# A four-layer kernel on one core: scatters moved behind a branch, gate weights loaded in attention, routing in pairs, folds reordered

## The chip, the cores and the metric

The program runs on one core of a Trainium2 chip. A core has a matrix engine (TensorE, here PE, with its weight loads PEld), a vector engine (VectorE, DVE), a scalar engine (ScalarE, ACT), a general engine (GpSimd, POOL) and an engine that issues transfers (SyncE, SP). Each follows its own list of instructions in order and waits on semaphores for the others. Transfers are issued on the queues of SP, ACT and POOL and run on 16 DMA engines that all queues share. The metric is the device time of one execution in microseconds (us). Before the change it is 3014.77 us, the median of three runs (3004.94 to 3015.94).

## The reference

The input is two sequences of 1024 tokens with 512 features. Four layers follow one another, each after a layer normalisation and added to its input:

```
x = x + attention(norm(x))        # 16 heads of 32, causal
x = x + experts(norm(x))          # 32 experts of inner width 192, the best 8 a token
x = x + state_space(norm(x))      # 16 heads, chunks of 64
x = x + feed_forward(norm(x))     # width 1376, weights looked up in a table of 16 values

# experts:
sel_w, sel_e = top_k(x @ gate_w.T, 8)
sel_w = softmax(sel_w)
h = silu(x @ w_gate[e].T) * (x @ w_up[e].T)
out = sum over the 8 of sel_w * (h @ w_down[e].T)
```

## The kernel before

All is done in 32-bit floats. Tokens stand in 16 blocks of 128 (`x_sb`), blocks 0 to 7 of sequence 0 and 8 to 15 of sequence 1.

**Attention** works in eight groups of four heads: groups 0 to 3 of sequence 0, groups 4 to 7 of sequence 1. Within a group, `scores` makes the score tiles of one block of keys, ACT takes their exponentials (`pT`), POOL masks the diagonal tiles, `values` multiplies by the values. Beside it, `maxima` makes the scores of the *next* group a first time, for their largest values only; `fold` turns these maxima (a DVE reduction into `nm`, four PE transposes `nm_ps`, ACT copies into spare rows of the queries) so that later scores come out with the maximum subtracted. `project_qk` makes the queries and keys of the group after the next, in four steps of 8 products each, evicted by DVE and ACT in turn. In this stage the order on PE, DVE and ACT is as written by hand: the generators are advanced one step at a time in `group`. The other queues, and everything outside attention, are ordered by a planner that goes by the order in which the program is traced and by its own idea of when things are ready. At the end of a group come one step of the projection, what is left of the maxima, the first fold, the last values, two steps of the projection, the second fold, the last step.

`normalise` makes a sequence's normalised features, and has POOL add the output bias to `x_sb`. At the start (`first_groups`) the first half of sequence 0 is normalised and projected before the second half. `clear_some` sends zeros to the scatter's destination during attention.

**Routing** (`_Router`): `route` takes some blocks, writes them to the accumulator, normalises, multiplies by the router, takes the best eight, and works out for each token and place a row number in `rows`, where each expert has 640 rows. `send` scatters the blocks' normalised rows to `rows`, one indirect DMA on POOL for each block and place. Places are ordered so that the first place holds the token's highest expert. A token that finds its expert full is handled apart: `finish` sets `over` if there is any, all five engines read it, and a branch (`tc.If`) runs `_left_over`. Sequence 0 is routed within attention (`route_first`). Sequence 1 is routed in `route_last`, two groups of four blocks, along with the last output projection: 64 scatters, all of them traced ahead of the branch.

**Experts** (`_sparse_experts`) go from 31 down to 0. `load_rows` fetches an expert's 640 rows, and waits for those places that can hold it (the first place for expert 31, the first two for 30, and so on). Five transposes turn them, `gates` makes 48 products with the gate weights `wgu`, `down` makes up to ten with `wd` and ACT's scaled result `y` (6 buffers) is added to the accumulator by an indirect DMA on POOL (line 988). Beside the experts DVE looks up the feed-forward weights (`_look_up`), and SP fetches the weights of the state space layer (`fetch`). Weights of the experts are loaded two experts ahead (`_expert_weights`); those of the first two are asked for after attention.

The **state space** layer and the **feed-forward** follow; the change doesn't touch them. A table of the former, `tri`, is loaded on ACT's queue (line 1145), and the planner puts that load ahead of ACT's first copies for the experts.

Of the kernel before, what the change touches and what calls it, by code (L numbers as in the profile page):

```python
# [18 lines left out]
P = 128  # L19
# [21 lines left out]
CAPB = 5  # L41
# [60 lines left out]
class _Router:  # L102
# [147 lines left out]
    def send(self, routed, places):  # L250
        tc = self.tc
        blocks, xr, idx = routed
        for k in places:
            for i, blk in enumerate(blocks):
                t = tc.nc.gpsimd.indirect_dma_start(  # L255
                    out=self.rows[:, :],
                    out_offset=bass.IndirectOffsetOnAxis(ap=idx[:, i, k : k + 1], axis=0),
                    in_=xr[i], in_offset=None,
                )
# [24 lines left out]
def _attention(tc, g, x_sb, a, router):  # L284
# [14 lines left out]
    with ExitStack() as ctx:  # L299
# [22 lines left out]

        load_x(range(TBLK // 2))
        load_w("wq", "wq")
        load_w("wk", "wk")
# [7 lines left out]

        bqs = wp.tile([P, NG], F32, tag="bqs", name="bqs")
        nc.vector.tensor_scalar(bqs, bqk[:, 0, :], DH**-0.5, None, ALU.mult)
# [44 lines left out]
        def normalise(b):  # L380

            for grp in range(TBLK // 4):
                blocks = range(b * TBLK + grp * 4, b * TBLK + grp * 4 + 4)
                norms = _norms(nc, g, x_sb, blocks)
                yield
                nc.vector.reciprocal(norms[1], norms[1])
                before = None
                for i, blk in enumerate(blocks):
                    xn = _normed(nc, x_sb, i, blk, norms, rp, ("row", ROW))
                    if before:  # L390
                        _turn(nc, g, *before, xnT, ps_f, "f")
# [27 lines left out]
        def project_qk(i):  # L419
# [4 lines left out]
            for hf in range(2):  # L424
                tok = slice(hf * 512, (hf + 1) * 512)
                for s, (dst, wn) in enumerate(((q, "wq"), (k, "wk"))):
                    pq = ps_f.tile([P, 512], F32, tag="f", name="pq")
                    for cc in range(NCC):
                        nc.tensor.matmul(
                            pq,  # L430
                            lhsT=w[wn][:, cc, gi * P : (gi + 1) * P],
                            rhs=xnT[:, cc, hf * 512 : (hf + 1) * 512],
                            start=cc == 0,
                            stop=cc == NCC - 1,
                        )
# [80 lines left out]
        def fold(i, hf):  # L516
# [8 lines left out]
            )  # L525
            pt = ps_s.tile([P, 4, P], F32, tag="s", name="nm_ps")
# [141 lines left out]
        def route_last(y):  # L668

            sk = ctx.enter_context(tc.tile_pool(name="rt_wk", bufs=1))  # L670
            psum = ctx.enter_context(tc.tile_pool(name="rt_ps", bufs=2, space=PSUM))

# [37 lines left out]
        def first_groups():  # L710


            norm, first = normalise(0), project_qk(0)
            for _ in range(6):
                next(norm)
            for _ in range(2):
                next(first)
                for _ in range(2):
                    next(norm)
            run(norm)  # L720
            run(first)
# [4 lines left out]
            fold(0, 0)  # L726
            run(other)
            fold(0, 1)
            load_w("wo", "wvo")

        def group(i, beside, sending):
# [55 lines left out]
            if follows:  # L787
                fold(i + 1, 1)
# [26 lines left out]
        route_last(y)  # L815
# [40 lines left out]
def _expert_weights(tc, a, pool):  # L856
# [5 lines left out]
    def load(e):  # L862
# [12 lines left out]
        wd = pool.tile([P, 2, D], F32, tag="wd", name="wd", bufs=3)  # L875
        src = a["wd"][e // 2]
        nc.sync.dma_start(out=wd[:, 0, :], in_=src[:, e % 2 * 2, :])
        tail = src[e % 2 * HB : (e % 2 + 1) * HB, 1, :]
        for r in (0, HB):
            nc.sync.dma_start(out=wd[r : r + HB, 1, :], in_=tail)  # L880
        return wgu, wd
# [4 lines left out]
def _sparse_experts(tc, g, a, router, ffn_w, load, loaded, fetch):  # L886
# [8 lines left out]
    with ExitStack() as ctx:  # L895
# [6 lines left out]
        wk = pool("se_wk", 2)  # L902
        ps_g = pool("se_ps_g", 4, PSUM)
# [8 lines left out]
        def load_rows(e):  # L912
            xg = wk.tile([P, CAPB, ROW], F32, tag="xg", name="xg")
            got = nc.sync.dma_start(
                out=xg,
                in_=rows[1 + e * CAP : 1 + (e + 1) * CAP, :].rearrange("(n p) d -> p n d", p=P),
            )

            needed = [s for sent in router.sent for s in chain(*sent[: E - e])]
            for s in needed:  # L920
                _after(tc, got, s)
            tc.declare_no_dep(
                got.ins, group="sent", keep=[s.ins for s in needed],
                reason="the other places hold no row of this expert",
            )
            return xg

# [76 lines left out]
        came = [load_rows(e) for e in order[:2]]  # L1004
# [4 lines left out]
        for n, e in enumerate(order):  # L1009
            wgu, wd = loaded[n]  # L1010
# [16 lines left out]
            if n + 2 < E:  # L1027
                loaded.append(load(order[n + 2]))
# [491 lines left out]
def kernel(ctx: ExitStack, tc: tile.TileContext, a: dict, out: bass.AP):  # L1520
# [26 lines left out]
    with tc.tile_pool(name="tokens", bufs=1, side="right") as tok:  # L1547
        x_sb = tok.tile([P, NBLK, D], F32, tag="x", name="x_sb")
        router = _Router(tc, g, x_sb, a, pool, rows, acc, left, [])
        _attention(tc, g, x_sb, a, router)  # L1550
        ew = first.enter_context(tc.tile_pool(name="se_w", bufs=1, reuse_waits="tile"))
        load = _expert_weights(tc, a, ew)
        loaded = [load(e) for e in (E - 1, E - 2)]
        some = nc.values_load(router.over[0:1, 0:1], min_val=0, max_val=1)
        with tc.If(some > 0):
            _left_over(tc, g, x_sb, a, left, acc[0])

# [22 lines left out]
    _sparse_experts(tc, g, a, router, ffn_w, load, loaded, fetch())  # L1580
# [106 lines left out]
```

## Time and profile before

| what | us |
|---|---|
| median of three runs | 3014.77 |
| the profiled execution | 3022.81 |
| its span, first to last instruction | 3020.7 |
| PE busy in the span | 2787.6 (92%) |
| DVE busy | 1382.0 (46%) |
| ACT busy | 928.1 (31%) |
| POOL busy | 632.6 (21%) |
| last output projection of attention ends | 829.2 |
| first product of the experts starts | 924.8 |

The profile is of one execution. A row of the timeline gives the start and the duration, the engine (a q behind it stands for its queue or sequencer), the line of the kernel, the operation, what it writes and reads, the shape and how many are drawn together, and in brackets how long the engine had been idle and what ended that. A row of the waits has who waited for whom, the total in us, the times and the longest. Starts of PE are measured and its ends are modelled. A row for one tile or line has the least, median and largest duration in ns, and the first and last start.

### The profile page before, as it was taken

The numbers are of one execution on the slowest core, as the hardware profiler recorded it, in microseconds if no ns is written. First come the engines' busy times: TensorE is split into PE (matmuls) and PEld (weight loads), VectorE is DVE, ScalarE is ACT, GpSimd is POOL, SyncE is SP. The second block draws the span as 40 slices with busy tenths as digits, with TensorE's granted clock in tenths as the row PEclk, the third lists the DMA queues.
The fourth block names the chain that finished last, engine by engine and source line by source line (L and its number), as shares of the span: only waits on it lengthen the run. The fifth ranks groups of instructions, "written<-read, shape, count | busy, mean of one in ns | idle before, by whom it ended". The sixth has DMA issues, their size and how long they took to land. (4 is left out here: it accounts for less than half of the span.)

```text
span 3020.7 us, 34117 instructions
## 1 busy us (share of the span) xinstructions
PE 2787.6 (92%) x11848; PEld 1624.7 (54%) x11848; DVE 1382.0 (46%) x3836; ACT 928.1 (31%) x1873; POOL 632.6 (21%) x786
## 2 busy tenths in 40 slices
PE   7998999989917999999999799999999997999999
PEld 3444444444414555555555378777777774444444
DVE  5555543545316999998111135545554454011010
ACT  1344432434302333333333234444444342100010
POOL 3022210423363334333333301101111010000000
PEclk9999999999858999999999889999999997999999
DMA  2466421212278988787877611111111132000000
GB/s 107 121 178 172 148 92 48 72 45 77 95 266 283 255 191 198 187 180 171 185 167 167 108 33 26 40 43 29 42 41 36 30 103 87 0 0 32 20 9 25
DMA packets 237685, 310.31 MB, mean 103 GB/s; under 512 B 60001, under 2 KB 126561, under 8 KB 236481
## 3 DMA queue, kind: packets, MB, share of 16 engines
q1 hardware_dynamic: 202928, 229.53, 24.9%
q0 software_dynamic: 33280, 77.68, 13.1%
q8 instruction: 97, 1.59, 0.2%
q10 hardware_dynamic: 1296, 0.83, 0.1%
q14 instruction: 84, 0.68, 0.1%
HBM read 159.12 MB, written 148.85 MB: 102 GB/s over the span
## 5 line engine op out<-in xcount | busy, mean ns | idle before, releaser
L944 PE MATMUL pg<-xgT,wgu 128*128 128x320 f32 x1536 | 469.2, 450 | 1.5 <-issue 1.5
L988 POOL DMA_INDIRECT acc<-y,tok x160 | 272.7, 1704 | 524.9 <-ACT y L987 364.3
L944 PEld LDWEIGHTS pg<-xgT,wgu 128*128 128x128 f32 x1536 | 285.1, 195 | 171.3 <-issue 61.6
L848 DVE SCALAR_TENSOR_TENSOR acc<-hit,lut,acc 128x688 f32<-128x688 bf16 (+2 forms) x405 | 345.3, 855 | 5.3
L1241 PE MATMUL pf<-xT,win 128*128 128x256 f32 x1024 | 242.5, 385 | 4.7 <-ACT gate L1269 3.9
L490 PE MATMUL sp<-ka,qa 64*128 64x512 f32 (+3 forms) x768 | 209.0, 514 | 6.5 <-DVE mx L511 3.2
L594 ACT ACTIVATE pT<-st 128x512 f32<-128x512 f32 (+3 forms) x384 | 158.2, 498 | 182.2 <-PE st L581 158.9
L1241 PEld LDWEIGHTS pf<-xT,win 128*128 128x128 f32 x1024 | 187.0, 190 | 38.0 <-PE pf L1241 6.0
L581 PE MATMUL st<-qa,ka 64*128 64x512 f32 (+3 forms) x768 | 177.4, 500 | 2.6 <-issue 1.9
L511 DVE TENSOR_REDUCE mx<-sp 128x1 f32<-128x384 f32 (+3 forms) x352 | 167.3, 492 | 16.9 <-PE sp L490 16.7
L1501 PE MATMUL pg<-xT,wg 128*128 128x512 f32 (+1 forms) x352 | 159.1, 595 | 0.0
L1510 DVE TENSOR_TENSOR hT<-s,pu 128x512 f32<-128x512 f32 (+1 forms) x44 | 30.3, 688 | 281.1 <-PE pu L1501 281.1
L1501 PE MATMUL pu<-xT,wu 128*128 128x512 f32 (+1 forms) x352 | 158.2, 592 | 0.0
L598 POOL TENSOR_SCALAR_AFFINE_SELECT pT<-pT 128x128 f32<-128x128 f32 x256 | 83.0, 337 | 347.7 <-ACT pT L594 335.5
L974 PE MATMUL po<-wd,hT 128*128 128x512 f32 x320 | 153.3, 593 | 1.6 <-ACT y L987 1.6
L612 PE MATMUL y<-pT,v 128*64 128x512 f32 (+3 forms) x768 | 149.7, 524 | 3.8 <-issue 2.9
L1483 PE MATMUL po<-wd,hT 128*128 128x512 f32 (+1 forms) x352 | 152.6, 592 | 0.0
L987 ACT ACTIVATE y<-po,rw 128x512 f32<-128x512 f32 x160 | 104.0, 685 | 155.4 <-PE po L981 151.1
L935 PE MATMUL xg_ps<-ident,xg 128*128 128x128 f32 x640 | 98.3, 278 | 57.2 <-issue 57.2
L255 POOL DMA_INDIRECT rows<-row,idx x128 | 126.1, 985 | 111.0 <-issue 71.3
L490 PEld LDWEIGHTS sp<-ka,qa 64*128 64x128 f32 x768 | 91.8, 187 | 94.7 <-issue 50.0
L981 PE MATMUL po<-wd,hU 64*128 64x512 f32 x320 | 126.0, 647 | 16.4 <-DVE hU L961 16.4
(190 smaller groups left out, 3822.9 us busy)
## 6 DMA issues: line engine op xcount, KB each, us to landing
rows<-blank SPq DMA_DIRECT2D x160, 272.5 KB
xg<-rows SPq DMA_DIRECT2D x32, 1362.5 KB
csb<-cs_rows SPq DMA_DIRECT2D x128, 128.0 KB
wgu<-in_wg_dram SPq DMA_DIRECT2D x32, 256.0 KB
wgu<-in_wu_dram SPq DMA_DIRECT2D x32, 256.0 KB
wd<-in_wd_dram SPq DMA_DIRECT2D x32, 256.0 KB
wd<-in_wd_dram SPq DMA_DIRECT2D x64, 128.0 KB
x<-x SPq DMA_DIRECT2D x32, 256.0 KB
```

What stands on the lines that cost most here:

```text
L490: nc.tensor.matmul(sp[hh][:, c0:c1], lhsT=q[half, pr, tb * P : (tb + 1) * P], rhs=k[half, pr, k0 * P : k1 * P], start=True, stop=True,)
L511: nc.vector.tensor_reduce(m[:, n : n + 1], sp[hh][:, c0:c1], AX.X, ALU.max)
L581: nc.tensor.matmul(st[:, c0:], lhsT=k[half, j // 2, kb * P : (kb + 1) * P], rhs=q[half, j // 2, qt * 512 + c0 : (qt + 1) * 512], start=Tru ...
L594: e = nc.scalar.activation(pT[:, c0:], st[:, c0:], AF.Exp)
L612: nc.tensor.matmul(y[j // 2][half, c0:], lhsT=v[:, kb, h // 2, h % 2 : h % 2 + 2, :].rearrange("p k d -> p (k d)"), rhs=ps[j][:, c0:], sta ...
L848: nc.vector.scalar_tensor_tensor(acc, hit, lut[:n, k : k + 1], acc, ALU.mult, ALU.add)
L944: nc.tensor.matmul(pg, lhsT=wgu[:, cc, m * P : (m + 1) * P], rhs=xgT[:, cc, cols], start=cc == 0, stop=cc == NCC - 1,)
L974: nc.tensor.matmul(o, lhsT=hT[:, j * P : (j + 1) * P], rhs=wd[:, 0, :], start=True, stop=False,)
L988: nc.gpsimd.indirect_dma_start(out=acc[turn[0] % 2][:, :], out_offset=bass.IndirectOffsetOnAxis(ap=tok[:, j : j + 1], axis=0), in_=y, in_o ...
L1241: nc.tensor.matmul(pf, lhsT=w[wn][:, cc, c0 : c0 + P], rhs=xT[st][:, cc], start=cc == 0, stop=cc == NCC - 1,)
L1483: nc.tensor.matmul(po, lhsT=hT[:n, fc, j * P : (j + 1) * P], rhs=wd[:n, fc, :], start=fc == 0, stop=fc == NFC - 1,)
L1501: nc.tensor.matmul(dst[:n, :], lhsT=w[:, cc, fc * P : fc * P + n], rhs=xT[:, cc, :], start=cc == 0, stop=cc == NCC - 1,)
```

## The change

- The scatters of sequence 1 are split. Blocks 8 to 11, 12 and 13, and 14 and 15 are routed as three parts (before: two groups of four blocks). Ahead of the branch two, two and one place of them are sent, 8 + 4 + 2 = 14 scatters. `route_last` returns the other 50, which are traced behind the branch, in the order of places.
- The gate weights and the others of an expert are parted. `wgu` tiles (two) are made before attention; there they hold the first 384 columns of `wq` and of `wk`, whose last 128 columns have tiles of their own. From group 6 on, the tiles take the gate weights of experts 31 and 30. `wd` is loaded within `_sparse_experts`.
- The first expert's rows come in five transfers of 128 rows each.
- `fold` becomes a generator with a pause behind its reduction. At the end of a group the rest of the maxima comes first, then the first reduction, a step of the projection, the first transposes, the second reduction, the last values, two steps, the second transposes, the last step.
- At the start all eight blocks of sequence 0 are normalised ahead of the first projection, and the scaling of the query bias (`bqs`) stands behind it. The output bias is added beside group 0 (sequence 0) and group 3 (sequence 1), by POOL.
- In `route_last` the scatters are no longer ordered behind the last mask.

```diff
@@ _Router.send
-                _after(tc, t, self.mask, mybir.DependencyClass.NoSync)
+                if self.mask is not None:
+                    _after(tc, t, self.mask, mybir.DependencyClass.NoSync)
@@ _attention
+        def load_qk(n):
+
+            w[n] = (
+                gates.tile([P, NCC, 2 * I], F32, tag="wgu", name=n, bufs=2),
+                wp.tile([P, NCC, P], F32, tag=n, name=n),
+            )
+            for t, c in zip(w[n], (0, 2 * I)):
+                nc.sync.dma_start(out=t, in_=a[n][:, :, c : c + t.shape[2]])
+
         load_x(range(TBLK // 2))
-        load_w("wq", "wq")
-        load_w("wk", "wk")
+        load_qk("wq")
+        load_qk("wk")
...
@@ normalise
                     before = xn, blk % TBLK
+                    yield
+                _turn(nc, g, *before, xnT, ps_f, "f")
+                yield
+
+        def output_bias(b):
+            for blk in range(b * TBLK, (b + 1) * TBLK):
+                tc.keep_in_program_order(
                     nc.gpsimd.tensor_tensor(
                         x_sb[:, blk, :], x_sb[:, blk, :], bvo[:, 1, :], ALU.add
                     )
-                    yield
-                _turn(nc, g, *before, xnT, ps_f, "f")
+                )
                 yield
@@ fold
                 mxs[i][:, t0 : t0 + 4], AX.X, ALU.max, negate=True,
             )
+            yield
             pt = ps_s.tile([P, 4, P], F32, tag="s", name="nm_ps")
@@ route_last
+            router.mask = None
...
             out = project_out(1, y)
-            routed, routing = [], iter(())
-            for grp in range(2):
-                for _ in range(4):
-                    next(out)
-                    routed += advance(routing)
-                    routed += advance(routing)
-                while len(routed) < grp:
-                    routed += advance(routing)
-                if grp:
-                    run(router.send(routed[0], range(4)))
-                blocks = range(TBLK + grp * 4, TBLK + grp * 4 + 4)
-                routing = router.route(blocks, sk, row_of, bank)
+            active, routed = [], []
+            parts = {3: range(8, 12), 5: range(12, 14), 7: range(14, 16)}
+            places = (2, 2, 1)
+
+            def advance_all():
+                for r in list(active):
+                    done = advance(r)
+                    if done:
+                        active.remove(r)
+                        run(router.send(done[0], range(places[len(routed)])))
+                        routed.extend(done)
+
+            for tb in range(TBLK):
+                next(out)
+                for _ in range(2):
+                    advance_all()
+                if tb in parts:
+                    sk = ctx.enter_context(tc.tile_pool(name=f"rt_wk{tb}", bufs=1))
+                    active.append(router.route(parts[tb], sk, row_of, bank))
             run(out)
-            while len(routed) < 2:
-                routed += advance(routing)
-            run(router.send(routed[1], range(4)))
-            for r in routed:
-                run(router.send(r, range(4, TOPK)))
+            while active:
+                advance_all()
             router.finish(bank)
+            return [
+                (r, [k]) for k in range(TOPK) for r, n in zip(routed, places) if k >= n
+            ]
@@ first_groups
-            norm, first = normalise(0), project_qk(0)
-            for _ in range(6):
-                next(norm)
-            for _ in range(2):
-                next(first)
-                for _ in range(2):
-                    next(norm)
-            run(norm)
-            run(first)
+            run(normalise(0))
+
+            nc.vector.tensor_scalar(bqs, bqk[:, 0, :], DH**-0.5, None, ALU.mult)
+            run(project_qk(0))
@@ group
+            run(more)
+            first, second = (fold(i + 1, hf) if follows else iter(()) for hf in range(2))
+            next(first, None)
             next(ahead, None)
-            run(more)
-            if follows:
-                fold(i + 1, 0)
+            run(first)
+            next(second, None)
             one(len(blocks) - 1)
             for _ in range(2):
                 next(ahead, None)
-            if follows:
-                fold(i + 1, 1)
+            run(second)
             run(ahead)
@@ the loop over groups
-                if i == 2:
+                if i == 0:
+                    beside = output_bias(0)
+                elif i == 2:
                     beside = normalise(1)
+                elif i == 3:
+                    beside = output_bias(1)
+                elif i == 6:
+                    for e in (E - 1, E - 2):
+                        load_gates(e)
@@ _sparse_experts
-        came = [load_rows(e) for e in order[:2]]
+        came = [load_rows(order[0], CAPB)]
+        wds = [load_down(order[0])]
+        came.append(load_rows(order[1]))
+        wds.append(load_down(order[1]))
@@ tile_preln_layers_kernel
-        _attention(tc, g, x_sb, a, router)
-        ew = first.enter_context(tc.tile_pool(name="se_w", bufs=1, reuse_waits="tile"))
-        load = _expert_weights(tc, a, ew)
-        loaded = [load(e) for e in (E - 1, E - 2)]
+        gates = first.enter_context(tc.tile_pool(name="se_w", bufs=1))
+        loaded = {}
+        load_gates = _expert_gates(tc, a, gates, loaded)
+        rest = _attention(tc, g, x_sb, a, router, gates, load_gates)
         some = nc.values_load(router.over[0:1, 0:1], min_val=0, max_val=1)
         with tc.If(some > 0):
             _left_over(tc, g, x_sb, a, left, acc[0])
+        for routed, places in rest:
+            for _ in router.send(routed, places):
+                pass
```

More of the change, by code (lines that the diff above doesn't have):

```diff
@@ L281, in _after, with _attention @@
     )
-def _attention(tc, g, x_sb, a, router):
+def _attention(tc, g, x_sb, a, router, gates, load_gates):
     nc = tc.nc
@@ L334, in _attention @@
         bqs = wp.tile([P, NG], F32, tag="bqs", name="bqs")
-        nc.vector.tensor_scalar(bqs, bqk[:, 0, :], DH**-0.5, None, ALU.mult)
         bvo = wp.tile([P, 2, D], F32, tag="bvo", name="bvo")
@@ L430, in project_qk @@
                             pq,
-                            lhsT=w[wn][:, cc, gi * P : (gi + 1) * P],
+                            lhsT=w[wn][gi // 3][:, cc, gi % 3 * P : (gi % 3 + 1) * P],
                             rhs=xnT[:, cc, hf * 512 : (hf + 1) * 512],
@@ L668, in route_last @@
         def route_last(y):
-            sk = ctx.enter_context(tc.tile_pool(name="rt_wk", bufs=1))
             psum = ctx.enter_context(tc.tile_pool(name="rt_ps", bufs=2, space=PSUM))
+            router.mask = None
             def bank(tag, shape):
@@ L725, in first_groups @@
                     next(other)
-            fold(0, 0)
-            run(other)
-            fold(0, 1)
+            run(fold(0, 0))
+            run(fold(0, 1))
             load_w("wo", "wvo")
@@ L814, in _attention @@
         inner.close()
-        route_last(y)
+        return route_last(y)
 def _look_up(tc, g, a, pool, lut, ffn_w):
@@ L853, in _look_up, with _expert_gates @@
             yield
-def _expert_weights(tc, a, pool):
+def _expert_gates(tc, a, pool, loaded):
     nc = tc.nc
@@ L874, in load, with _sparse_experts @@
             )
[L875 to L881, printed above, removed]
+        loaded[e] = wgu
     return load
-def _sparse_experts(tc, g, a, router, ffn_w, load, loaded, fetch):
+def _sparse_experts(tc, g, a, router, ffn_w, load_gates, loaded, fetch):
     nc = tc.nc
@@ L902, in _sparse_experts @@
         wk = pool("se_wk", 2)
+        dw = pool("se_wd", 3)
         ps_g = pool("se_ps_g", 4, PSUM)
@@ L910, in _sparse_experts, with load_rows, load_down @@
         look_up = _look_up(tc, g, a, lk, lut, ffn_w)
-        def load_rows(e):
+        def load_rows(e, parts=1):
             xg = wk.tile([P, CAPB, ROW], F32, tag="xg", name="xg")
[L914 to L917, printed above, removed]
             needed = [s for sent in router.sent for s in chain(*sent[: E - e])]
[L920 to L925, printed above, removed]
-            return xg
+            src = rows[1 + e * CAP : 1 + (e + 1) * CAP, :].rearrange("(n p) d -> p n d", p=P)
+            for n in range(0, CAPB, CAPB // parts):
+                part = slice(n, n + CAPB // parts)
+                got = nc.sync.dma_start(out=xg[:, part], in_=src[:, part])
+                for s in needed:
+                    _after(tc, got, s)
+                tc.declare_no_dep(
+                    got.ins, group="sent", keep=[s.ins for s in needed],
+                    reason="the other places hold no row of this expert",
+                )
+            return xg
+        def load_down(e):
+            wd = dw.tile([P, 2, D], F32, tag="wd", name="wd")
+            src = a["wd"][e // 2]
+            nc.sync.dma_start(out=wd[:, 0, :], in_=src[:, e % 2 * 2, :])
+            tail = src[e % 2 * HB : (e % 2 + 1) * HB, 1, :]
+            for r in (0, HB):
+                nc.sync.dma_start(out=wd[r : r + HB, 1, :], in_=tail)
+            return wd
         def transpose(xg, t):
@@ L1009, in _sparse_experts @@
         for n, e in enumerate(order):
-            wgu, wd = loaded[n]
+            wgu, wd = loaded[e], wds[n]
             xgT, tok, rw = t
@@ L1027, in _sparse_experts @@
             if n + 2 < E:
-                loaded.append(load(order[n + 2]))
+                load_gates(order[n + 2])
+                wds.append(load_down(order[n + 2]))
                 came.append(load_rows(order[n + 2]))
@@ L1578, in fetch @@
         yield
-    _sparse_experts(tc, g, a, router, ffn_w, load, loaded, fetch())
+    _sparse_experts(tc, g, a, router, ffn_w, load_gates, loaded, fetch())
     first.close()
```

## The prediction

> **What bounds the kernel now.** I read the windows first (busy time in stretches of 50 us), then the waits of TensorE (PE), then the order of time where PE stands still. Outside 830 to 950 us PE is 90 to 100% busy: attention up to 829 us, experts from 925 to 1722, the state space layer, the feed-forward. So time is to be won only where PE waits, or by less PE work; the change removes none of the latter.
>
> ```profile
> 850.00:900.00 50.00, 5.99 (x26) 5.48 (x26) 5.91 (x42) 0.31 (x1) 28.98 (x31) 0.50 0.72 245
> 900.00:950.00 50.00, 26.39 (x101) 17.75 (x102) 17.73 (x39) 11.52 (x19) 20.08 (x21) 0.73 0.77 269
> 950.00:1000.00 50.00, 47.95 (x171) 27.56 (x169) 46.92 (x88) 17.67 (x32) 17.72 (x10) 0.97 1.01 318
> ...
> PE xg_ps L935 <- issue: 57.2, 2, 36.7
> PE nm_ps L528 <- DVE nm L521: 35.3, 15, 3.4
> ...
> PE rt_p L200 <- DVE chosen L194: 17.4, 1, 17.4
> ```
>
> The windows' columns are PE, weight loads, DVE, ACT, POOL, PE's clock, the share of the DMA engines and GB/s. Between 850 and 900 only POOL works. Of the waits below, the first and third lie in this hole; the second is the folds, twice in each attention group.
>
> ```profile
> 833.50 0.98 POOL L255 DMA_INDIRECT rows<-row,idx  x1 [35.23 <-issue]
> ...
> 856.83 0.29 DVE L184 COPY logits<-rt_l 128x128 f32<-128x128 f32 x1 [21.21 <-remote]
> ...
> 865.66 0.96 POOL L255 DMA_INDIRECT rows<-row,idx  x1 [11.94 <-DVE miss L244]
> ...
> 883.49 1.94 PE L935 MATMUL xg_ps<-ident,xg 128*128 128x128 f32 x8 [20.59 <-issue]
> ...
> 919.04 0.34 ACTq L1145 DMA_DIRECT2D tri<-in_consts_dram  x1
> ...
> 922.08 2.91 PE L935 MATMUL xg_ps<-ident,xg 128*128 128x128 f32 x12 [36.65 <-issue]
> ```
>
> ```profile
> L275 DVE TENSOR_SCALAR over<-most x1: 124/124/124, 864.5 to 864.5; 128x1 int32<-128x1 f32 x1
> ...
> L1554 ACTq TENSOR_LOAD <-over x1: 466/466/466, 864.7 to 864.7; - x1
> ...
> L1554 POOLq TENSOR_LOAD <-over x1: 507/507/507, 918.5 to 918.5; - x1
> ```
>
> The hole read forwards: the first expert's rows are there at 883.5, PE turns two banks, and then needs ACT's copies. ACT stands at the load of `tri` (919.04), half a microsecond after POOL has read `over` (918.5). The other engines read it at 864.7 to 865.4. POOL came late because 58 of the 64 row scatters of the last tokens stood ahead of its read, at 1.27 us from one to the next. I take it that `tri` lies where `over` lay and waits for all its readers; that the times meet supports this. The first expert product starts at 924.78. Of the 17.4 us before it (841.5 to 858.9), DVE waits for the end of PE's router product, whose end is modelled at 841.5, while weights and 16 scatters fill the DMA engines (share 0.82 from 842 to 859). Why it took so long the profile doesn't say.
>
> **The change, part by part.**
>
> *Scatters and branch.* POOL has 8+4+2 = 14 scatters ahead of the branch in place of 58 (of 64). Routing of the last pair can start at 829.2, with the last output projection. Copied from the group of four before: statistics at 832, normalised rows from 833.5; two rows instead of four 834.6; transposes and copies two by 836.6 (four took to 838.5); 16 of 32 router products 838.5; logits to indices 7.7 us for four, I take 6 for two: 844.5. This leaves out the wait of 15 us behind a full DMA, since the gate weights are loaded long before and scatters alone remain. POOL: 833.5 + 14 x 1.27 = 851.3, later than the indices, so POOL sets it. It reads `over` at 852. The last of the 14 starts at 850; the last scatter of the burst of 16 (852.8) signalled at 857.2, so 4.4 us: 854.5. The 1.36 MB of rows took from 874.4 to 882.3 with scatters beside; in five parts PE can turn each as it lands, so 862.5 + 2.5 = 865 instead of 924.8: **60 us gained**. Three routings rather than two cost more small operations, in this estimate within the 6 us.
>
> *What the moved scatters cost.* 50 are left, behind the branch. They used to run while PE stood still; now they run beside the experts. POOL: the nearest row is the accumulating scatter, which runs beside DVE 98% busy (950 to 1420) and beside an idle DVE (1450 to 1690):
>
> ```profile
> L988 POOL DMA_INDIRECT acc<-y,tok x92: 1551/1754/2493, 953.1 to 1412.8; - x92
> ...
> L988 POOL DMA_INDIRECT acc<-y,tok x51: 1550/1551/1560, 1452.9 to 1684.6; - x51
> ...
> L255 POOL DMA_INDIRECT rows<-row,idx x64: 957/963/1202, 833.5 to 925.2; - x64
> ```
>
> Its mean is 1.82 against 1.55 us, a sixth more. So a row scatter takes 0.96 x 1.17 + 0.31 = 1.43 us, and 50 take 72 us, to 927 (3.3 us lie between POOL's branch and its next scatter). All the experts' accumulating scatters queue behind them. The first `y` comes 27.4 us after the first product (952.2 against 924.8), the seventh 49 us after it (973.3 is the seventh), so at 914; there are 6 `y` buffers, and ACT would stand for 13 us, with copies and Silus behind it, then PE. The Trainium skill speaks harder against this. "SBUF — State Buffer", section "SBUF: two separate sides", says that GpSimd can't write its DMA descriptors while DVE holds the port that they share, and the section after it ("A bandwidth-pool intuition that's wrong") puts such a DMA at about 620 ns alone and 3100 ns beside a DVE copy, five times. By that rule a scatter takes 0.96 x 5 + 0.31 = 5.1 us and 50 take 255; ACT would stand for 196 us. The row shows a sixth, not five times, with the same look-up on DVE; I take the row.
>
> DMA: in 886 to 922 the scatters took 0.73 us of all 16 engines each (27 scatters, 62% of 32 us), so 50 are 36 us of full DMA. The first four experts' stretches in the old trace (925 to 1021) already had shares of 0.90, 0.95, 1.07 and 0.92. "DMA: Bandwidth & Descriptors", section "Issuing engines are not separate DMA queues", says that all queues end on the same 16 engines; shares that add to 1.5 then delay rows and weights by what doesn't fit. Bounds: 36 us if nothing hides it; 0 if it is taken from the 11 MB of the next layer's weights, which are fetched then and not needed before 1730. Rows are two experts ahead at most, and share SP's queue with that fetch. I take **20 us lost**, for this and POOL's 13 together, as they fall into the same stretch: a late PE makes `y` late too. Rows for expert n need 2 + 8(n-1) of the 50, 11 us an expert against 24 us each takes, so the order itself starves nobody. `wd` now lands behind the rows, needed some 20 us later: hidden; without that cover 0.5 MB, under 2 us.
>
> *Folds.* Around the fold of group 0:
>
> ```profile
> 170.63 3.70 PE L429 MATMUL pq<-xnT,wq 128*128 128x512 f32 x8
> ...
> 177.00 0.63 PE L528 MATMUL nm_ps<-ident,nm 128*128 128x128 f32 x4 [2.67 <-DVE nm L521]
> ...
> 187.85 0.66 PE L528 MATMUL nm_ps<-ident,nm 128*128 128x128 f32 x4 [2.58 <-DVE nm L521]
> ```
>
> The reduction `nm` (0.22 us) stands on DVE behind four evictions of the projection just made, DVE and ACT in turn (0.74, 0.68). Now it is put ahead of them; the maxima end at 169.2 and the division at 171.9, before that projection ends at 174.3. So both waits go. There are 12 such (six groups, 32.1 us together); the pair of the first groups stays. What is late next: ACT's evictions keep their 3 us behind each projection; replaying group 0 the next scores start at 187.0 instead of 191.9, 4.9 us for 5.2. Six times that: **29 us gained**.
>
> *Start.* All tokens of the first sequence are normalised before its first projection. Tokens 4 to 7 land at 22.3 to 24.9, so their last copy is at 32, and four projections (5.9 us the first, at the low clock, 3.6 the others, as at 17.9) end at 48.8, against 47.4: **1 us lost**, between -1 and +3, the smaller pieces of `wq` and `wk` included.
>
> *At nothing:* eight bias additions per half on POOL (1.26 us each) leave the start and go beside groups 0 and 3, where POOL is 20 to 30% busy and each comes behind the masks that PE needs; if not covered, 10 us each. The gate loads at group 6 add 8 DMAs, 5 us of SP's queue, past blank rows that nothing waits for soon; DMA is at 0.2 there. Dropping the order against the mask frees POOL where no mask is left.
>
> **Sum:** -60 + 20 - 29 + 1 = -68. The profiled execution took 3022.8 (span 3020.7), so 2954.8; the median of the runs is 8.0 lower: **2947**.
>
> **The rivals.** (B) *The flood is hidden* by fetches that can wait: no 20 us, 2927. For it: DMA runs at up to 400 GB/s; against: shares near 1 already. (C) *The hole moves*: PE, let in early, stands behind the flood, as it did from 841 to 858 when scatters and weights met, or the planner still keeps POOL's read late; the 60 is eaten and the folds remain: 3014.8 - 28 = 2987. (D) *Nothing of it counts*, another wait takes each place: 3005 to 3015. (E) *Slower*, by POOL alone: scatters beside the look-up take d us each and every `y` waits. ACT stands from the seventh `y` (914) until 855 + 50 d. The gains are 88, so it decides from d = (59 + 88)/50 = 2.9 us; at the rule's 5.1, 196 us lost less 88: 3123. Against it is the 1.82.
>
> **How the numbers follow.** Likeliest case 0.50, 2947 (2928 to 2966); B 0.17; C 0.20; D 0.05; E 0.08. What a measurement tells from no change is about 0.5%, 15 us. Faster: 0.50 + 0.17 + 0.20 + 0.02 = 0.89; same 0.03; slower 0.08. The range leaves out E, D and the far ends of B and C: 2912 to 2992.
>
> **What would show it.** POOL's read of `over` near 852 and the first expert product near 865; rows' scatters 1.4 us apart until 925, the first accumulating one after them; DMA share about 1 for the first four experts with PE idle some 20 us in all, waiting for rows or for `y`; no `nm_ps` wait on DVE in groups 0 to 5. Wrong it is if the first product comes after 890, if scatters take over 2 us each, or if `nm_ps` still waits.

## The result and the profile after

The changed kernel takes **2969.75 us**, the median of four runs (2967.35 to 2978.29), the kernel before beside it 3011.31 us (3004.94 to 3015.94): a ratio of **0.9869** (95% interval 0.9839 to 0.9898), 41.6 us less. The forecast was 2947, in a range of 2912 to 2992. The profiled execution took 2978.29 us, its span is 2976.6 us against 3020.7: 44 us less, where the sum of steps said 68.

First the windows of the changed kernel, in the columns of those before (PE, weight loads, DVE, ACT, POOL, PE's clock, DMA share, GB/s), then its waits of PE:

```profile
800.00:850.00 50.00, 19.37 (x66) 13.37 (x65) 4.22 (x32) 4.47 (x7) 33.67 (x36) 0.58 0.83 293
850.00:900.00 50.00, 15.80 (x47) 9.49 (x47) 11.85 (x23) 7.40 (x13) 22.79 (x24) 0.62 0.55 206
900.00:950.00 50.00, 48.64 (x179) 27.88 (x178) 47.57 (x95) 17.27 (x31) 17.99 (x10) 1.00 1.04 313
```

```profile
PE xg_ps L964 <- ACT xgT L965: 21.7, 1, 21.7
PE xg_ps L964 <- DMA xg<-rows: 20.8, 1, 20.8
...
PE pg L973 <- issue: 15.4, 7, 2.7
...
PE nm_ps L543 <- DVE nm L535: 4.4, 4, 2.6
```

The last line is the folds: 35.3 us in 15 waits before, 4.4 in 4 now. The other lines are a hole that is still there, only earlier: PE is busy 35 of the 100 us from 800 to 900. POOL now reads `over` at 810.9 with the other engines (918.5 before), and experts start at 833.1 (924.8 before). But look at what PE does then. First its timeline, then that of the others:

```profile
833.12 5.38 PE L973 MATMUL pg<-xgT,wgu 128*128 128x320 f32 x16
841.03 0.63 PE L964 MATMUL xg_ps<-ident,xg 128*128 128x128 f32 x4 [2.54 <-issue]
844.39 4.48 PE L973 MATMUL pg<-xgT,wgu 128*128 128x320 f32 x8 [2.73 <-issue]
...
854.24 0.43 PE L973 MATMUL pg<-xgT,wgu 128*128 128x320 f32 x1 [2.36 <-issue]
857.04 0.69 PE L973 MATMUL pg<-xgT,wgu 128*128 128x320 f32 x1 [2.37 <-issue]
...
865.44 0.69 PE L973 MATMUL pg<-xgT,wgu 128*128 128x320 f32 x1 [2.11 <-issue]
887.82 1.12 PE L964 MATMUL xg_ps<-ident,xg 128*128 128x128 f32 x4 [21.68 <-ACT xgT L965]
```

```profile
843.75 0.59 ACT L965 COPY xgT<-xg_ps 128x512 f32<-128x512 f32 x1 [7.84 <-remote]
...
864.09 1.28 ACT L979 ACT_TABLE_LOAD   x1 [19.75 <-remote]
...
878.84 0.96 POOL L255 DMA_INDIRECT rows<-row,idx  x1 [0.30 <-issue]
...
884.42 0.49 DVE L981 TENSOR_TENSOR hT<-s,pg 128x320 f32<-128x320 f32 x1 [43.16 <-remote]
...
902.10 1.79 POOL L1017 DMA_INDIRECT acc<-y,tok  x1 [22.30 <-ACT y L1016]
```

From 850 PE starts one matmul in 2.8 us (with its weight load between, one instruction in 1.4). The starts run ahead of the work; how fast PE works is seen from those who wait for it. PE's signal for the last transposes of expert 31 comes at 843.73, for its first product (8 matmuls, 8 weight loads) at 864.03, for its second at 884.34: 20.3 us for 16 instructions, 1.27 us each. POOL's scatters start 1.27 us apart. In the steady experts such a product takes 2.3 us. ACT, DVE and then PE itself wait for these signals. The last scatter starts at 878.84, and by 888 PE runs without stops again. I call this **the hold**. PE's clock isn't its reason, since from 850 to 855 the full clock was granted and PE still did two matmuls in 5 us:

```profile
850.00:855.00 5.00, 0.86 (x2) 0.37 (x2) 0.00 (x0) 0.00 (x0) 3.78 (x5) 1.00 1.03 383
```

Nor does PE seem to lack instructions: of the transfers that fetch them, those of 16 KB come once in some 250 instructions of PE (236 to 259 in five long stretches of this trace). They come twice behind the branch (812.6 and 816.0) and next at 905.6, when PE has long gone on. Expert 31 takes 61 us, against 17 before. (Here and below an expert is timed by the row copies `rw` of its two successors, each made at the same place of the expert before: for expert 31 from those of 30 to those of 29.)

Stages from the traces, in us, from start to start: cut at the first and the last score product (`st`), the first expert product, the row copy of the seventh expert and that of the last. Chips differ, so runs on one chip stand together.

| kernel | to first score | attention | to first product | first experts | other experts | rest |
|---|---|---|---|---|---|---|
| before | 114.0 | 677.1 | 133.6 | 110.5 | 615.7 | 1369.7 |
| after | 106.6 | 644.8 | 81.8 | 157.1 | 616.8 | 1369.5 |

7.4 us come from the start, 32.3 from attention, 51.8 from the earlier first product; the first experts give 46.6 of it back.

### The profile page after: what moved, and what is told of

Same layout as the page of the kernel before. It is cut to its first block, busy times and chain, and to the rows that moved or that the text cites. A ratio compares the mean times of both kernels' runs of the same rounds, so it can differ in the third digit from the quotient of the medians.

```text
span 2976.6 us, 34151 instructions
## 1 busy us (share of the span) xinstructions
PE 2785.1 (94%) x11848; PEld 1626.1 (55%) x11848; DVE 1378.8 (46%) x3849; ACT 929.3 (31%) x1875; POOL 632.8 (21%) x786
## 5 line engine op out<-in xcount | busy, mean ns | idle before, releaser
L525 DVE TENSOR_REDUCE mx<-sp 128x1 f32<-128x384 f32 (+3 forms) x352 | 167.2, 492 | 17.6 <-PE sp L504 17.1
```

The costliest lines, as they stand in the source:

```text
L525: nc.vector.tensor_reduce(m[:, n : n + 1], sp[hh][:, c0:c1], AX.X, ALU.max)
```

## The experiments

My theory after the result: the run of 50 scatters on POOL holds PE (theory S), so that what the branch's earlier read gained is lost in expert 31. The rival L: DMA engines at a share of 1.03 to 1.05 hold it, by loads of which many could come later.

**One chip: parts of the change.** The folds alone on the kernel before:

```diff
@@ fold
             )
+            yield
             pt = ps_s.tile([P, 4, P], F32, tag="s", name="nm_ps")
@@ group
-            next(ahead, None)
             run(more)
-            if follows:
-                fold(i + 1, 0)
+            first, second = (fold(i + 1, hf) if follows else iter(()) for hf in range(2))
+            next(first, None)
+            next(ahead, None)
+            run(first)
+            next(second, None)
             one(len(blocks) - 1)
             for _ in range(2):
                 next(ahead, None)
-            if follows:
-                fold(i + 1, 1)
+            run(second)
...
```

> The kernel before with the folds alone changed: reduction ahead of the features' products, transposes behind them. Forecast: 29 us less, 2982. By the marks of the changed kernel's trace (last score product 39.8 us earlier, of which 8 at the start): 32 less, 2979. If part of it is owed to the bias adds moved off POOL: 2985 to 2995.

Measured: 2945.46 us against 2986.06, ratio 0.9867 (0.9834 to 0.9900). The folds alone give as much as the whole change gave in its first measurement, and more than expected (40.6 us less, where 29 or 32 were). PE's waits in that kernel show that the folds' waits go without the bias additions, which stay where they were:

```profile
PE nm_ps L529 <- DVE nm L521: 4.4, 4, 2.6
```

All 64 scatters ahead of the branch again, in the changed kernel:

```diff
@@ route_last
+            for k in range(TOPK):
+                for r, n in zip(routed, places):
+                    if k >= n:
+                        run(router.send(r, [k]))
             router.finish(bank)
-            return [
-                (r, [k]) for k in range(TOPK) for r, n in zip(routed, places) if k >= n
-            ]
+            return []
```

> The changed kernel with all 64 scatters of the last tokens ahead of the read of the overflow flag again, in the order by place, all else as changed. As forecast (scatters ahead cost 60, behind 20): 3005 to 3012. Theory S (the hold only moves with the scatters): the flag read at about 875, the first product at 890 to 895, no hold in expert 31, 2965 to 2980.

Measured: 2958.24 us, ratio 0.9891 (0.9857 to 0.9924). Beside the folds alone on the same chip this is 13 us more (of medians), though the start is 4 us shorter: three routings, five parts of the first rows and early gate weights win nothing while POOL reads `over` at 854.0. The intervals overlap. The profiled executions lie 27 us apart; 12 of these are in the first experts, the others are spread over the later stages. My numbers in us were for another set of runs, so only ratios can be set side by side: 3005 to 3012 would be 0.998 to 1.000 of before, 2965 to 2980 (theory S) 0.985 to 0.990. So the forecast's view of this kernel fails, and the number is near theory S; but S had the hold in mind, which this chip doesn't seem to have (see the fourth chip).

The 50 scatters left out, so that the later places of the last tokens are never written:

```diff
-        for routed, places in rest:
-            for _ in router.send(routed, places):
-                pass
```

> The changed kernel without the 50 scatters behind the branch: they are left out, so the later places of the last tokens are never written and the experts compute on stale rows of the same shape. Theory S (the run of scatters on POOL holds TensorE): expert 31 takes 18 to 24 us in place of 63, the time falls from 2970 by 40 to 48 to 2922 to 2930. Rival L (the loads for the experts, up to 1.05 of the DMA engines, hold it): at least 20 us of the 40 stay, 2945 to 2970.

Measured: 2893.68 us, ratio 0.9683 (0.9658 to 0.9709). By ratio that is below both theories (2922 to 2930 would be 0.970 to 0.973). In its windows no hole is left, though the DMA share is as high:

```profile
800.00:850.00 50.00, 45.37 (x185) 30.46 (x186) 32.99 (x69) 19.23 (x33) 8.60 (x5) 0.90 0.99 304
850.00:900.00 50.00, 48.40 (x164) 27.01 (x162) 44.70 (x86) 14.39 (x26) 15.79 (x10) 0.93 1.05 312
```

The same scatters spread over the experts, two after each of the products, each place ahead of the load that needs it:

```diff
+            sends = sending(n + 2)
             for i, _ in enumerate(gates(e, xgT, wgu, hT, hU)):
                 next(turning, None)
+                for _ in range(2):
+                    next(sends, None)
```

> The changed kernel with the same 50 scatters, two at a time between the products of experts 31 to 26, each place just ahead of the load that needs it. Theory S with a long unbroken run as the condition (bursts of 3 beside attention's and the experts' products held nothing): expert 31 takes 18 to 30 us, 2925 to 2940. If every scatter takes its 1.27 us from TensorE wherever it stands, the 50 cost what they cost now: 2965 to 2975. Rival L: as now, 2965 to 2975.

Measured: 2930.97 us, ratio 0.9816 (0.9788 to 0.9844). By ratio this lies between the theories (2925 to 2940 would be 0.971 to 0.976, 2965 to 2975 would be 0.985 to 0.988). Expert 31 takes 22 us, as S had it, but experts 30 to 26 take 26 to 32 each, and these five add up to 142 us, where they take 112 without scatters. What I lacked was the changed kernel on this chip: whether there was a hold to be taken away here, in this run or in the one before, was not known.

| kernel | to first score | attention | to first product | first experts | other experts | rest |
|---|---|---|---|---|---|---|
| folds alone | 111.2 | 626.5 | 120.0 | 108.2 | 613.0 | 1361.0 |
| scatters ahead | 106.8 | 630.8 | 122.9 | 120.3 | 617.5 | 1368.9 |
| left out | 105.6 | 629.8 | 73.7 | 108.4 | 620.8 | 1359.2 |
| spread | 107.0 | 621.7 | 69.9 | 142.5 | 618.5 | 1361.4 |

**A second chip: the changed kernel again, and fewer loads.** The spread's result suggested a theory D: among the first experts the DMA engines are the bound, and the scatters' bytes are their cost. Loads that no early expert needs (wb, wc, win, wout, and the table's `idx`) are made to wait for the rows of the eighth and later experts (`LATE` is 6):

```diff
@@ _look_up
+        if m < 2:
+            _after(tc, got, marks[-1])
@@ _sparse_experts
-                for _ in range(2):
+                for _ in range(3 if n >= LATE else 0):
                     next(look_up, None)
...
-            next(look_up, None)
-            next(fetch, None)
+            if n >= LATE:
+                next(look_up, None)
+                got = next(fetch, None)
+                if got:
+                    _after(tc, got, marks[-1])
```

> The changed kernel as it is, beside the others of this call on one chip, so that its stages can be set against theirs. If its first runs are typical: 0.987 of before.

> The kernel before as it is, for a trace from the same chip. Theory S+D (folds give all of the gain, the transition and the first experts together give nothing): from the last score product to the last expert's rows it takes 855 to 862 as in the changed kernel, whichever chip. If the chip sets it: near 840, as in the kernel with the folds alone.

> The changed kernel with its 50 scatters in one run, and with the loads that no early expert needs (wb, wc, win, wout, and the table's idx) held back to the seventh expert on. Theory S (scatters hold TensorE): the hold in expert 31 stays at 40 us or more; what is gained (up to 15) lies in experts 30 to 26. Rival L (full DMA engines hold it): expert 31 shrinks from 63 us to 25 to 35, and the time by 28 to 40.

> The scatters spread as in the run before, and the same loads held back to the seventh expert on. Without the scatters the experts took 729 us, with them spread 761: 32 more, near 50 x 0.73 us of all DMA engines = 36. Theory D (in the first six experts the DMA engines are the bound, and each byte more is time): 20 to 32 of these come back, ratio to before 0.971 to 0.975. Rival (the scatters' cost isn't their bytes): no change, 0.980 to 0.983.

Measured: the changed kernel 2913.65 us against 2991.90, ratio **0.9764** (0.9712 to 0.9817); with the loads late 0.9749 (0.9715 to 0.9783); spread with the loads late 0.9836 (0.9801 to 0.9870); the kernel before one execution of 2989.62 us.

| kernel | to first score | attention | to first product | first experts | other experts | rest |
|---|---|---|---|---|---|---|
| before | 114.2 | 660.6 | 121.4 | 108.6 | 619.7 | 1362.4 |
| after | 105.6 | 623.4 | 77.3 | 131.8 | 615.6 | 1360.6 |
| after, loads late | 106.9 | 628.1 | 76.3 | 106.8 | 631.1 | 1358.0 |
| spread, loads late | 106.9 | 624.6 | 73.2 | 128.8 | 641.2 | 1358.0 |

Here the same program has almost no hold, so that S and L, which both said what would become of expert 31's 60 us, can't be told apart on this chip: expert 31 takes 20 us. Beside the same run of scatters a product takes PE 2.3 us until 849.85, and then it stands for 8.9 us. PE's timeline of the changed kernel on this chip:

```profile
823.63 2.32 PE L973 MATMUL pg<-xgT,wgu 128*128 128x320 f32 x8
...
847.43 2.42 PE L973 MATMUL pg<-xgT,wgu 128*128 128x320 f32 x8
858.73 1.11 PE L964 MATMUL xg_ps<-ident,xg 128*128 128x128 f32 x4 [8.88 <-ACT xgT L965]
```

The kernel before agrees. In the trace shown ahead of the prediction DVE waits 21.21 us for PE's router product beside scatters; here it waits 5.82. DVE's timeline of the kernel before on this chip:

```profile
824.99 0.29 DVE L184 COPY logits<-rt_l 128x128 f32<-128x128 f32 x1 [5.82 <-PE rt_l L180]
```

So my expectation for the kernel before (855 to 862 from the last score product to the last rows) fell: the cut gives 849.8, and the changed kernel wins 25.0 there: 44 by the earlier product, less 23 in the first experts, and 4 in the others.

Without a hold the scatters' cost is another one. With the loads late the first experts fall from 131.8 to 106.8, less than before's 108.6, with the 50 scatters still in one run, and with a DMA share down from 1.08 to 0.89 between 850 and 900. Windows of the kernel with the loads late:

```profile
800.00:850.00 50.00, 40.15 (x154) 26.54 (x155) 4.19 (x15) 14.03 (x24) 37.81 (x41) 0.85 1.02 373
850.00:900.00 50.00, 48.70 (x186) 28.23 (x184) 5.49 (x16) 16.55 (x30) 25.19 (x19) 1.00 0.89 214
```

That is as D has it; but as DVE has next to nothing to do in these two rows, this run alone doesn't tell whether the bytes or DVE's look-up crowded the experts. The late look-up then costs 15.5 us in the other experts, so that the time is hardly better (with the fetch alone late, below, they cost nothing more). Spread with the loads late, which D put at 0.971 to 0.975, did worse than the run of scatters: 128.8 us in the first experts where one run takes 106.8, and 641 in the others, for which I have no cause.

**A third chip: the hold by itself.** Scatters of the same number that move an eighth of the bytes (64 of 545 numbers of a row, to a place of their own of 36865 x 64; the later places stay unwritten), and only the later layer's weights held back:

```diff
@@ send
-                    out=self.rows[:, :],
+                    out=to[:, :],
...
-                    in_=xr[i], in_offset=None,
+                    in_=xr[i][:, : to.shape[1]], in_offset=None,
```

```diff
@@ _sparse_experts
-            next(fetch, None)
+            if n >= 6:
+                got = next(fetch, None)
+                if got:
+                    _after(tc, got, marks[-1])
```

> The changed kernel as it is, beside the next two on one chip. In its first profile expert 31 took 63 us, in its second 20. If that goes with the chip, the ratio to before is 0.976 with about 20 us, or 0.987 with about 60.

> The changed kernel with the 50 scatters behind the branch writing 64 of the 545 numbers of each row, to a place of their own: as many instructions and descriptors, an eighth of the bytes; the later places of the last tokens stay unwritten, as when they were left out. Theory D (the bytes beside the loads are the cost): from the first product to the seventh expert's rows about 108 to 114 us in place of 132, expert 31 near 20, ratio 0.968 to 0.971. Theory S (POOL's run of scatters, whatever they move): 125 to 132 where expert 31 takes 20, over 150 where it takes 60; ratio as the changed kernel's.

> The changed kernel with only the layer's loads behind the experts (wb, wc, win, wout) held back to the seventh expert on, the table's look-up left where it was. Theory D: the first seven experts' 132 us fall to 108 to 115 as when both were held back, and the later experts don't pay the 15 us that the delayed look-up cost them (631 in place of 616): ratio 0.968 to 0.972. Rival (it was idx, or the look-up's work on DVE, that crowded the first experts): as the changed kernel, 0.975 to 0.978.

Measured against 3006.14 us: the changed kernel 2959.36, ratio 0.9849 (0.9820 to 0.9878); narrow 0.9840 (0.9817 to 0.9863); with the fetch late 0.9813 (0.9789 to 0.9838). The last has 6.5 us less in the first experts than the changed kernel, and its interval overlaps with the latter's.

| kernel | to first score | attention | to first product | first experts | other experts | rest |
|---|---|---|---|---|---|---|
| after | 106.3 | 632.2 | 80.7 | 155.6 | 616.9 | 1363.4 |
| narrow | 106.6 | 638.8 | 76.9 | 163.4 | 618.8 | 1359.6 |
| after, fetch late | 106.6 | 635.5 | 78.0 | 149.1 | 614.5 | 1361.9 |

The hold is back, 62 us for expert 31, and narrow settles what it isn't. Windows of that kernel, then the end of its run of scatters and ACT's first operations behind it:

```profile
830.00:850.00 20.00, 6.36 (x17) 2.87 (x15) 0.00 (x0) 1.72 (x2) 15.12 (x17) 0.63 0.48 166
850.00:870.00 20.00, 0.00 (x0) 0.00 (x0) 0.49 (x1) 0.00 (x0) 15.12 (x17) 0.50 0.08 26
870.00:890.00 20.00, 11.16 (x29) 7.72 (x30) 10.12 (x20) 4.10 (x8) 4.96 (x5) 0.59 0.03 9
```

```profile
874.72 1.46 POOL L256 DMA_INDIRECT narrow<-row,idx  x1 [0.30 <-issue]
...
882.88 0.44 ACT L980 ACTIVATE s<-pg 128x320 f32<-128x320 f32 x1 [10.67 <-remote]
```

From 850 to 870 the DMA engines are 8% busy, ACT stands, DVE does one operation of 0.49 us, POOL does 17 scatters, and no product starts on PE. (Its clock of 0.50 goes with its standing, as between 850 and 900 in the kernel before.) So it is neither the bytes nor the loads (rival L, and theory D for this chip): expert 31 takes 68 us with an eighth of the bytes and 61 with the fetch late. In all four traces of the changed kernel and its variants with a hold PE runs without stops again 5 to 10 us after the last scatter starts: 878.8 and 887.8, 866.1 and 873.8, 868.5 and 873.9, 874.7 and 883.9.

**A fourth chip: spread, with only the fetch late.**

> The scatters spread over experts 31 to 26 (14 in one run behind the branch, then 2 to 6 at a time), and the layer's later weights held back to the seventh expert on. On a chip where the changed kernel's expert 31 takes 60 us: if only a long unbroken run of scatters holds TensorE, expert 31 takes 20 to 30 and the time is 0.970 to 0.978 of before; if each scatter costs TensorE 1.27 us wherever it stands, the first seven experts take 150 as now, 0.981 to 0.985. On a chip where expert 31 takes 20: the first seven take 115 to 130 in place of 142 with the spread alone, 0.972 to 0.978.

Measured: 2940.35 us against 3007.40, ratio 0.9785 (0.9761 to 0.9808).

| kernel | to first score | attention | to first product | first experts | other experts | rest |
|---|---|---|---|---|---|---|
| spread, fetch late | 105.9 | 638.4 | 73.9 | 137.1 | 619.5 | 1362.8 |

Expert 31 takes 20 us, experts 30 to 26 take 27 to 30 each; the ratio lies just outside the 0.970 to 0.978 that went with such an expert 31. Whether this chip holds PE at all was not seen, since the changed kernel didn't run on it; the kernel before has the time that it has where the hold was seen (3011, 3006; without it 2986, 2992).

The traces have a second mark. The 64 scatters of sequence 0, in attention, are in every kernel, and where the records are whole each lands with 16 signals. Of these 1024 signals the traces of the second chip and of the chip on which the parts were run (the parts' chip) record 1018 to 1024; those of the first pair, of the third chip and of this one record 542 to 584. The full hold was seen only where signals are missing. The view of these scatters gives their time to landing only where the records are whole. First the changed kernel on the second chip, then the kernel on this one, which has no such line:

```profile
L255 POOL DMA_INDIRECT rows<-row,idx x64: 956/960/1461, 499.9 to 734.1; - x64
DMA to landing us min/median/max: 2.8/3.1/5.0
```

```profile
L255 POOL DMA_INDIRECT rows<-row,idx x64: 956/960/1459, 500.4 to 749.5; - x64
```

By this mark the fourth chip is of the kind that holds PE, and the parts' chip isn't, so that the parts' runs had no hold to take away. If the mark holds, this version beats both kernels on such chips (0.9785 against 1 and against the changed kernel's 0.9849 and 0.9869); where PE isn't held the changed kernel as it is has the lower ratio (0.9764), and on the spread's first chip it wasn't measured. The DMA share is 0.82 to 0.87 here, so full DMA engines are not the whole reason why the first experts take 137 us with spread scatters and 108 without (the latter on the parts' chip). Windows of this kernel:

```profile
800.00:850.00 50.00, 35.23 (x140) 23.73 (x141) 22.71 (x53) 15.57 (x26) 17.16 (x18) 0.80 0.82 256
850.00:900.00 50.00, 38.46 (x135) 22.08 (x134) 27.29 (x54) 12.13 (x22) 27.06 (x20) 0.90 0.87 232
```

## Why the prediction was right or wrong

The sign, the range and most steps held; the sum missed by 24 us (44 in place of 68 in the profiled executions), and the likeliest case, 2928 to 2966, was missed too. Against the forecast the start gave 8 us more and the folds 3, the branch 8 less, and the moved scatters cost 27 more. The step that failed is this last one. That the time fell inside the range was partly luck, since the start's gain was not foreseen and made up for part of it.

- **Folds, 29 us.** Attention got 32.3 us shorter in the first pair of traces, 37.2 on the second chip, and 34 between the kernel before there and the folds alone, on the parts' chip. The step was right: of 12 `nm_ps` waits on DVE in groups 0 to 5 one was left, of 1.1 us in group 5, where none was forecast.
- **Start, 1 us lost.** Wrong in sign: 7.4 us gained (8.6 on the second chip). The failed step is "Tokens 4 to 7 land at 22.3 to 24.9, so their last copy is at 32". By the landing signals in the trace before they were there by 15.7 to 17.6. Their statistics were late because DVE works in the written order and stood waiting for the first projection's products. DVE's timeline before:

```profile
23.84 0.74 DVE L447 TENSOR_SCALAR qa<-pq,bqk 32x512 f32<-32x512 f32 x1 [7.82 <-PE pq L429]
25.32 0.74 DVE L447 TENSOR_SCALAR qa<-pq,bqk 32x512 f32<-32x512 f32 x1 [0.75 <-ACT qa L442]
26.10 0.69 DVE L68 BATCH_NORM_STATS2 ln_st<-x_sb 128x6 f32<-128x512 f32 x1
```

  In the trace after they follow the first half's without a pause. DVE's timeline after:

```profile
8.91 7.99 DVE L79 TENSOR_SCALAR ln_xn<-x_sb,ln_mv,ln_rs 128x512 f32<-128x512 f32 x4
16.82 0.67 DVE L68 BATCH_NORM_STATS2 ln_st<-x_sb 128x6 f32<-128x512 f32 x1
```

  The first projection starts at 25.0, and the four end at 39.4 in one run, the first of 4.2 us and the others of 3.6, where 48.8 was forecast.
- **Scatters and branch, 60 us gained.** 51.8 from the last score product to the first expert product; 44.1 on the second chip, where the kernel before lacked its own hold in the routing. POOL's read came 23.4 us after the end of the last output projection, as forecast (22.8). From there to the first product it took 22.2 us in place of 13: the first rows were asked for at 818.9, behind three loads of `wd` (from 816.3), where the forecast had `wd` land behind the rows, and PE got the last of them at 832.2, beside the scatters. The stretch from 841 to 858 in the kernel before, of which I wrote that the profile doesn't say why it took so long, looks like the same hold, and I counted on it to go.
- **What the moved scatters cost, 20 us.** This term was mis-sized: it is 46.6 us. It was built from POOL's and the DMA engines' time, with PE waiting some 20 us for rows or for `y`. What came was the hold: PE, with rows and weights there, finished one instruction in 1.27 us until the run of scatters ended, and expert 31 alone took 44 us more. Rival C had named it: "PE, let in early, stands behind the flood, as it did from 841 to 858". It let all of the 60 be eaten, for 2987; by mechanism C came true, and the start's gain, which no case had, brought the time back towards the likeliest case. On the second chip the term was 23 us, the sum came to 73 us in the spans (2987.1 to 2914.3) where 68 was forecast, and the likeliest case was right there. (The row of `y` was misread by one, without consequence: 973.3 is the sixth, 974.9 the seventh.)
- **Scatters slower beside DVE.** In the hold DVE stood, and a scatter kept its 0.96 us, so the first trace didn't test it. Spread over the experts, with DVE at 65 to 75%, they took 1.14 us on average, and 0.97 with the look-up late and DVE at 8 to 10%: beside DVE a fifth more, near the sixth that I took from the row. It is far from the fivefold of the Trainium skill's "SBUF — State Buffer", section "A bandwidth-pool intuition that's wrong (but worth ruling out)", which is stated for a DVE `tensor_copy`, while DVE's look-up here has other operations. Rival E is out. In the trace no `y` waited for a buffer.
- **At nothing.** The bias additions cost nothing that shows: attention takes 626.5 us with the folds alone and 621.7 to 630.8 with the changed kernel's variants on that chip. `wd` ahead of the first rows is told above.

What stays open: how a run of scatters on POOL keeps PE to one instruction each, and why it did so in the first and the third set of runs of the changed kernel and not in the second. The second and third were on different chips; which chip the first was on is not known. That it goes with the chip rests on four executions in each set, within 0.9% of one another, on the kernel before, whose routing shows the same difference, and on the missing landing signals, which never differ between traces of one chip. Why they go with the hold is open. Each execution has its clock and span from the recorder, so whether the recording has a part in the hold wasn't tested. A hold and its absence were never seen on one chip with the scatters alone changed, so that spreading them takes the hold away is likely, by the mark of the fourth chip too, but not shown.

## What to carry to other kernels

Ask of each stall in a trace what else ran then, even where the profile names no releaser: the unexplained 17 us beside 16 scatters were a warning of what 50 would cost. Work that is taken out of one hole has to be given cover where it goes, and "another engine, and room on the DMA engines" is not cover until a trace shows the two side by side for as long. And where kernels are compared by one or two per cent, run them on the same chip, and on more than one; look for a mark in the traces that tells chips apart before an experiment is read.

## What the runs showed of the hardware

- Beside an unbroken run of indirect row scatters TensorE completed 16 instructions in 20.3 us, one per scatter of 1.27 us; on another chip it ran beside more than 40 of them at full pace and then stood for 8.9 us. With an eighth of the bytes, and DMA engines 8% busy from 850 to 870, the hold was no shorter (68 us for expert 31).
- Traces with a hold record 542 to 584 of the 1024 landing signals of 64 earlier scatters; those of the second chip and the parts' chip record 1018 to 1024.
- The same two programs stood at 0.9869, 0.9764 and 0.9849 in three sets of runs, the last two on different chips.
- On the second chip, without the hold, 50 scatters of some 0.73 us of all DMA engines each (the prediction's estimate) cost the first experts 23 us (131.8 against 108.4 without them on the parts' chip, 108.6 before), and nothing once loads and look-up came later (106.8).
